# Thirteen edge tiles for four runs of nodes, an earlier last product and a shorter finish in a two-layer graph kernel

## The chip, the cores and the metric

The kernel runs on one core of a Trainium2 chip. A core has five engines with queues of their own: TensorE (PE in the profile, its weight loads PEld), VectorE (DVE), ScalarE (ACT), GpSimd (POOL) and SyncE (SP). They work side by side and wait for each other through semaphores. The metric is device microseconds of one execution. Before the change the median of seven runs is 2106.64 us, the lowest 2105.11 and the highest 2107.53.

## The reference, cut to what matters

Two graph layers run over 6250 nodes of 512 numbers in fp32. There are 106,250 edges: 50,000 random pairs in both directions, and one loop per node. The edges come sorted by dst.

```python
edge_index = stack([src, dst])
# layer one
agg = segment_sum((x @ W_l.T + b_l)[src], dst)
x = layernorm(x + agg / max(deg, 1) + x @ W_r.T)
# layer two, sums by src, gathers by dst
neigh = segment_sum(h[dst] @ W_neigh.T + b_neigh, src) / max(deg, 1)
z = h + relu(h @ W_self.T + b_self + neigh)
x = layernorm(h + layernorm(z) * gamma + beta)
```

The products are linear, so the kernel sums the rows of neighbours first and multiplies the mean by the weight matrix once per node.

## The kernel before, in words

Each layer works on a list of edges sorted by the node that receives. The list is cut into tiles of 128 edges: 831 in layer one, 782 in layer two (whose one loop per node is left out of the list and added from the node's own row). A *window* is a run of at most 32 nodes. The class `Sorter` cuts the windows so that a pair of them owns a fixed number of edge tiles, `PAIR = 7` in layer one and `PAIR_L = 6` in layer two: 238 and 261 windows. `place` (L470) reads each window's first node from the sorted list with selector matmuls, writes it to `lo`, checks that no window is too wide, and writes `rel`: for every edge of each tile that a window visits, the node's place in the window.

A *group* is four windows, one from each quarter of the list (`C = 4`), with 32 of the 128 partitions each; `Q` is the number of groups, 60 in layer one and 66 in layer two. A tile that two windows share is gathered once and visited by both. `gathered` (L602) issues one indirect DMA on POOL's queue per tile, 128 rows of 2 KB each, into one of ten chunks of four tiles.

`grouped` (L616) is a software pipeline over the groups, in an order written out by hand. The iteration for group g puts the gathers of group g + 1 on POOL's queue (`fetch`) and builds that group's 0/1 matrix `hot` on DVE (`match`). PE then does the first two visits of group g, the transposes of the mean of group g - 1, the product of that group's own rows (`dense` "own", into the PSUM tile `po`), visit three, the mean's product into the same `po`, the transposes of group g's own rows, the rest of the visits and the degree. DVE and ACT make the mean (`average`). `close` runs the first half of the finish of group g - 1, and `store`, in the next iteration, the second half and the store. A visit (`visits`, L721) is a matmul of a tile's `hot` columns with the gathered rows; the four windows write four different quarters of the PSUM tile `agg`, and each fp32 matmul shows as two instructions. Own rows come by SP's queue (`begin`, L709) and results leave by it (L781), but for three groups near a layer's end, whose stores are indirect DMAs on POOL's queue (L774).

`po` has one buffer in layer one and two in layer two (`bufs=1 + layer`). The finish of layer one is `finish0` (L547), that of layer two `finish1` (L559). `both` (L178 is its line) is a DVE instruction over two tensors; `spread` gives the mean and the deviation, the latter on ACT, and `normalize` applies them. Layer two's list is sorted on DVE, ACT and PE during layer one, a few steps per group (`more`).

Of the kernel before, what the change touches and what calls it, by code (L numbers as in the profile page):

```python
# [18 lines left out]
P = 128  # L19
C = 4  # L20
H = P // C
PAIR = 7
PAIR_L = 6
CHUNKS = 10
# [74 lines left out]
def kernel(  # L99
# [53 lines left out]
    last, middle = [const.tile([P, P], F32, name=n) for n in ("last", "middle")]  # L153
    for t, row in ((last, P - 1), (middle, P // 2 - 1)):
        nc.vector.tensor_scalar(t, ones, pidx, None, op0=ALU.mult)
        nc.vector.tensor_scalar(t, t, float(row), None, op0=ALU.is_equal)

# [56 lines left out]
    class Sorter:  # L214


        def __init__(self, key, val, layer, pool, ps, loops, given=None):
# [6 lines left out]
            pair = self.pair = PAIR_L if loops else PAIR  # L224
            self.half = (pair + 1) // 2
            self.vis = self.half + 1
            self.NW = (2 * self.M + pair - 1) // pair

            self.Q = (self.NW + 2 * C - 1) // (2 * C) * 2
            Q = self.Q  # L230
# [10 lines left out]
            if loops:  # L241

                a = (E - N - CAP - 1) // P
                self.row = pool.tile([P, M - a], F32, name="row")
                nc.gpsimd.iota(self.row, pattern=[[P, M - a]], base=a * P - (E - N) + LOOP,
                               channel_multiplier=1, allow_small_or_imprecise_dtypes=True)
                self.more = const.tile([P, 1], F32, name="more")
                self.parts = 2 + (M - a - 1) // (W // CAP // 2 * 2)

# [136 lines left out]
        def first_rows(self):  # L386

            n = 1 + self.half
            self.first = const.tile([P, C, n], I32, name="first")
            for c in range(C):  # L390
                a = c * (self.Q // 2 * self.pair) - 1
                k = max(0, -a)
                v = self.val[(a + k) * P:(a + n) * P]
                nc.scalar.dma_start(self.first[:, c, k:], v.rearrange("(t p) -> p t", p=P))
# [75 lines left out]
        def place(self):  # L470

            lo, pad, Q, NW = self.lo, self.padded, self.Q, self.NW
            pair, half, vis = self.pair, self.half, self.vis
            mid = middle if pair % 2 else last
# [5 lines left out]
            ne, no = (NW + 1) // 2, NW // 2  # L480

            for a, sel, off, n in ((0, last, 0, ne), (D // 2, mid, half, no),
                                   (D, last, pair - 1, ne - 1), (D + D // 2, last, half - 1, no)):
                nc.tensor.matmul(ends[:, a:a + n], sel, bass.AP(
                    tensor=pad.tensor, offset=pad.offset + off,
                    ap=[list(pad.ap[0]), [pair, n]]), start=True, stop=True)
            nc.vector.memset(lo, float(N))
            nc.vector.tensor_copy(view(lo, (0, 2, ne, 1)), ends[:, :ne].unsqueeze(2))
            nc.vector.tensor_copy(view(lo, (1, 2, no, 1)),
                                  ends[:, D // 2:D // 2 + no].unsqueeze(2))  # L490
# [7 lines left out]
            nc.vector.tensor_tensor(bad[:, NW:NW + ne - 1].unsqueeze(2),  # L498
                                    view(one, (2, 2, ne - 1, 1)),
                                    ends[:1, D:D + ne - 1].unsqueeze(2), op=ALU.is_equal)  # L500
            nc.vector.tensor_tensor(bad[:, NW + ne - 1:2 * NW - 1].unsqueeze(2),
                                    view(one, (1, 2, no, 1)),
                                    ends[:1, D + D // 2:D + D // 2 + no].unsqueeze(2),
                                    op=ALU.is_equal)
# [7 lines left out]

            for c in range(C):
                for i, off in ((0, 0), (1, half)):
                    nodes = bass.AP(tensor=pad.tensor, offset=pad.offset + pair * Q // 2 * c + off,
                                    ap=[list(pad.ap[0]), [pair, Q // 2], [1, vis]])
                    rel = self.rel.rearrange("p (q i) v c -> p q i v c", i=2)[:, :, i, self.X:, c]
                    first = view(lo, (c * Q + i, 2, Q // 2, 1))
                    nc.vector.tensor_tensor(rel, nodes, first.to_broadcast([P, Q // 2, vis]),
                                            op=ALU.subtract)  # L520
# [26 lines left out]
    def finish0(nr, po, own, some, work):  # L547
        po = po[:nr]
        nc.vector.scalar_tensor_tensor(po, biases["bl"][:nr], some[:nr], po,
                                       op0=ALU.mult, op1=ALU.add)  # L550
        v = work.tile([P, D], F32, name="v", bufs=1)
        both(v[:nr], po, own[:nr], ALU.add)
# [6 lines left out]
    def finish1(nr, po, own, some, work):  # L559
        po = po[:nr]  # L560
        if some is None:
# [8 lines left out]
        normalize(po, po, mv, root, nr)  # L570
        both(po, po, biases["ga"][:nr], ALU.mult)
        both(po, po, biases["be"][:nr], ALU.add)
        y = work.tile([P, D], F32, name="y")
        both(y[:nr], po, own[:nr], ALU.add)
# [27 lines left out]
    def gathered(s, table, t, windows, idx):  # L602

        rows = rpool.tile([P, C, D], F32, name="rows", bufs=CHUNKS)
        got = {}
        for c in windows:
            m = c * (s.Q // 2 * s.pair) + t
            if 0 <= m < s.M:
                at = idx[:, m:m + 1] if idx is s.idx else idx[:, c, t + 1:t + 2]
                nc.gpsimd.indirect_dma_start(  # L610
# [377 lines left out]
```

## Time and profile before

| what | us |
|---|---|
| median of 7 runs | 2106.64 |
| the profiled execution | 2105.06 |
| its span | 2103.3 |
| PE busy | 1939.9 |
| POOL busy | 1556.7 |
| DVE busy | 1182.9 |
| first gather of layer one starts | 5.70 |
| last gather of layer one starts | 1063.09 |
| first gather of layer two starts | 1086.51 |
| last gather of layer two starts | 2071.27 |

The profile comes from one execution. A line of a group gives the source line, engine, operation, tiles out<-in, shapes and count; then busy us and mean ns of one; then the engine's idle time just before these instructions and what ended most of it. "issue" means that the engine waited for nothing that the profile shows. A line of the timeline gives start, duration, the instruction and its count; several like it in a row are merged (x3), and the idle time before it stands in brackets with what ended it. The granted TensorE clock was 0.987 of full speed on average.

### The profile page before, as it was taken

What the parts mean: (1) busy time and instruction counts of PE and PEld (TensorE: products, weight loads), DVE (VectorE), ACT (ScalarE), POOL (GpSimd) and SP (SyncE); (2) the same over time, 40 slices, a digit from 0 to 9 for tenths busy, and PEclk for the clock granted to TensorE, in tenths of its full rate; (3) what the DMA queues carried; (4) which work ended last, traced back from release to release, by engine and by line L of the source; (5) the groups of instructions that cost most, each with busy time, mean ns of one, the idle gap of its engine ahead of it and who ended that gap; (6) DMA issues with size and microseconds to landing.
All of it is one profiled execution on the core that took longest, in us unless ns stands there. A gap on an engine that the chain in (4) does not pass through costs nothing.

```text
span 2103.3 us, 26066 instructions
## 1 busy us (share of the span) xinstructions
PE 1939.9 (92%) x7723; PEld 669.0 (32%) x7723; DVE 1182.9 (56%) x2495; ACT 315.8 (15%) x661; POOL 1556.7 (74%) x1638
## 2 busy tenths in 40 slices
PE   4899999999999999999879999999999999999996
PEld 1333333333232333333223333333333333333332
DVE  4754555545455554343424656565656565666577
ACT  0111111111111111111101111111111111111111
POOL 7777777777777777777747777777777777777773
PEclk9999999999999999999989999999999999999999
DMA  8777777887888887777757888888888888878783
GB/s 265 229 231 240 234 238 238 239 243 232 246 252 254 252 246 240 238 241 237 232 151 225 244 243 246 245 246 243 246 244 245 246 244 244 247 243 247 242 247 116
DMA packets 186885, 498.49 MB, mean 237 GB/s; under 512 B 46562, under 2 KB 49052, under 8 KB 186726
## 3 DMA queue, kind: packets, MB, share of 16 engines
q0 software_dynamic: 130128, 426.11, 67.6%
q1 hardware_dynamic: 50228, 64.61, 9.6%
q10 hardware_dynamic: 6370, 5.94, 0.9%
q8 instruction: 65, 1.06, 0.2%
q14 instruction: 94, 0.77, 0.1%
HBM read 463.90 MB, written 32.96 MB: 236 GB/s over the span
## 4 chain that ended last, share of the span: by engine, by line
DMA 30%; POOL 28%; PE 25%; issue 14%; DVE 3%; SPq 0%; ACT 0%; POOLq 0%; ACTq 0%; DVEq 0%
POOL rows L610 28%; DMA rows<-h_d,idx 17%; DMA rows<-in_x_dram,idx 12%; PE po L599 11%; PE agg L721 10%; PE tp L591 3%; DMA rows<-in_x_dram,first 0%; DVE stats L533 0%; PE turn L296 0%; DVE po L178 0%; PE deg L730 0%; DMA first<-in_src_dram 0%; DVE agg L748 0%; DMA own<-in_x_dram,slots 0%; SPq L781 0%
## 5 line engine op out<-in xcount | busy, mean ns | idle before, releaser
L721 PE MATMUL agg<-rows,hot 128*32 128x512 f32 x4220 | 897.5, 615 | 106.4 <-DMA rows<-h_d,idx 42.4
L610 POOL DMA_INDIRECT rows<-in_x_dram,idx x815 | 783.1, 961 | 248.1 <-issue 209.3
L610 POOL DMA_INDIRECT rows<-h_d,idx x785 | 745.6, 950 | 241.5 <-issue 197.4
L599 PE MATMUL po<-wa,meanT 128*128 128x512 f32 (+1 forms) x1008 | 466.0, 605 | 0.0
L599 PE MATMUL po<-wb,ownT 128*128 128x512 f32 (+1 forms) x1008 | 453.5, 593 | 0.1
L721 PEld LDWEIGHTS agg<-rows,hot 128*32 128x32 f32 x4220 | 155.4, 109 | 625.9 <-DMA rows<-in_x_dram,idx 228.2
L582 DVE TENSOR_SCALAR inv<-deg 128x1 f32<-128x1 f32 (+1 forms) x60 | 9.5, 158 | 485.9 <-PE deg L730 478.0
L599 PEld LDWEIGHTS po<-wa,meanT 128*128 128x128 f32 (+1 forms) x1008 | 180.2, 188 | 286.7 <-issue 254.8
L599 PEld LDWEIGHTS po<-wb,ownT 128*128 128x128 f32 (+1 forms) x1008 | 180.7, 189 | 181.9 <-issue 181.6
L593 ACT COPY ownT<-tp 128x512 f32<-128x512 f32 (+1 forms) x126 | 73.2, 581 | 785.9 <-PE tp L591 776.3
L739 DVE TENSOR_SCALAR loops<-deg 128x1 f32<-128x1 f32 (+1 forms) x66 | 10.4, 158 | 310.6 <-PE deg L730 301.6
L178 DVE SCALAR_TENSOR_TENSOR srt<-srt 128x448 f32<-128x448 f32 (+3 forms) x313 | 181.1, 620 | 4.0
L752 ACT ACTIVATE mean<-agg,inv 128x512 f32<-128x512 f32 (+1 forms) x126 | 86.5, 687 | 338.9 <-DVE some L585 140.7
L661 DVE TENSOR_REDUCE hotb<-hot 128x128 bf16<-128x512 f32 (+1 forms) x126 | 133.7, 1061 | 0.1
L537 ACT ACTIVATE rstd<-mv,eps 128x1 f32<-128x1 f32 (+1 forms) x192 | 56.5, 294 | 433.8 <-DVE mv L535 430.6
L593 ACT COPY meanT<-tp 128x512 f32<-128x512 f32 (+1 forms) x126 | 73.1, 580 | 190.3 <-PE tp L591 190.3
L178 DVE SCALAR_TENSOR_TENSOR hot<-rel,cols 128x640 f32<-128x640 f32 x126 | 98.1, 778 | 0.0
L591 PEld LDWEIGHTS tp<-ident,own 128*128 128x128 f32 (+1 forms) x504 | 63.0, 142 | 79.8 <-issue 76.7
L591 PEld LDWEIGHTS tp<-ident,mean 128*128 128x128 f32 (+1 forms) x504 | 52.8, 141 | 110.9 <-issue 43.5
L591 PE MATMUL tp<-ident,own 128*128 128x128 f32 (+1 forms) x504 | 76.1, 274 | 12.2 <-DMA own<-in_x_dram,slots 6.5
L591 PE MATMUL tp<-ident,mean 128*128 128x128 f32 (+1 forms) x504 | 82.5, 287 | 4.4 <-ACT mean L752 4.4
L543 DVE TENSOR_SCALAR po<-po,mv,rstd 128x512 f32<-128x512 f32 (+1 forms) x66 | 54.0, 819 | 2.4
(152 smaller groups left out, 916.9 us busy)
## 6 DMA issues: line engine op xcount, KB each, us to landing
own<-h_d SPq DMA_DIRECT2D x261, 64.0 KB
out_dram<-y SPq DMA_DIRECT2D x250, 64.0 KB
own<-in_x_dram SPq DMA_DIRECT2D x230, 64.0 KB
h_d<-y SPq DMA_DIRECT2D x227, 64.0 KB
rows<-in_x_dram,idx POOLq DMA_INDIRECT x815
rows<-h_d,idx POOLq DMA_INDIRECT x785
wa<-in_L_gnn_W_l_dram ACTq DMA_DIRECT2D x4, 256.0 KB
wb<-in_L_gnn_W_r_dram ACTq DMA_DIRECT2D x4, 256.0 KB
```

The lines of the kernel that those rows point to most:

```text
L178: nc.vector.scalar_tensor_tensor(o, a, 1.0, b, op0=ALU.mult, op1=op)
L537: nc.scalar.activation(root[:nr], mv[:nr, 1:2], AF.Sqrt, bias=eps[:nr])
L543: nc.vector.tensor_scalar(y, v, mv[:nr, 0:1], root[:nr], op0=ALU.subtract, op1=ALU.mult)
L582: nc.vector.tensor_scalar(inv[:nr], deg, 1.0, None, op0=ALU.max)
L591: nc.tensor.transpose(p[:, k, :nr], v[:nr, k * P:(k + 1) * P], ident[:nr, :nr])
L593: nc.scalar.copy(t[:, :, :nr], p[:, :, :nr])
L599: nc.tensor.matmul(po[:nr], aT[:, k, :nr], w[:, k, :], start=first and k == 0, stop=end and k == NK - 1)
L610: nc.gpsimd.indirect_dma_start(out=rows[:, c, :], out_offset=None, in_=table, in_offset=bass.IndirectOffsetOnAxis(ap=at, axis=0))
L661: nc.vector.tensor_reduce(hb[:, 0, :], hots[g][:, s.X * C:n * C].rearrange("p (v c) h -> p (c h) v", c=C), axis=mybir.AxisListType.X, op=A ...
L721: nc.tensor.matmul(agg[H * c:H * (c + 1), :], hot[:, C * (s.X + v) + c, :], chunks[t][c], start=t == ts[0], stop=t == ts[-1])
L739: nc.vector.tensor_scalar(st["loops"][:nr], deg[:nr, 1:2], 1.0, None, op0=ALU.add)
L752: nc.scalar.mul(st["mean"][:nr], st["agg"][:nr], st["inv"][:nr])
```

## The change

In layer two four windows own 13 tiles, so that there are 241 windows in 61 groups. Layer one keeps two windows to 7 tiles and its 60 groups. In layer two the windows of a cycle begin at rows 127, 31, 63 and 95 of a tile; the first of the four visits five tiles and the others four, and since 61 is one more than a multiple of four, the four windows of a group stand at four different places of the cycle. The selector tiles become four, the copies and checks of `place` run over the places of the cycle, and `rel` has five visits per window, filled with -1 where there is none.

Gathered rows are kept in 40 tiles of their own rather than ten chunks of four. The last group of each layer issues its own rows' product at the end of its own iteration, behind its sums and after `close` of the group before, rather than in the extra iteration behind the transposes of its mean. `finish0` adds the scaled bias to the own rows in a tile `v` and then the product to it. `finish1` makes `add`, own rows plus `be`, ahead of the rest, and its affine part and the last sum are two instructions in place of four.

```diff
-PAIR = 7
-PAIR_L = 6
-CHUNKS = 10
+CYCLE = 2, 7
+CYCLE_L = 4, 13
+ROWS = 40
...
-    last, middle = [const.tile([P, P], F32, name=n) for n in ("last", "middle")]
-    for t, row in ((last, P - 1), (middle, P // 2 - 1)):
+    row_of = {}
+    for row in range(P // 4 - 1, P, P // 4):
+        t = row_of[row] = const.tile([P, P], F32, name=f"row{row}")
         nc.vector.tensor_scalar(t, ones, pidx, None, op0=ALU.mult)
         nc.vector.tensor_scalar(t, t, float(row), None, op0=ALU.is_equal)
+    last = row_of[P - 1]
...
-            self.NW = (2 * self.M + pair - 1) // pair
-
-            self.Q = (self.NW + 2 * C - 1) // (2 * C) * 2
-            Q = self.Q
+            n, T = self.cycle = CYCLE_L if loops else CYCLE
+            self.NW = (n * self.M + T - 1) // T
+
+            Q = self.Q = (self.NW + C - 1) // C
+
+
+            starts = [i * T * P // n - 1 for i in range(n + 1)]
+            self.at = [v // P for v in starts[:n]]
+            self.row_at = [v % P for v in starts[:n]]
+            self.num = [b // P - a // P + 1 for a, b in zip(starts, starts[1:])]
+            self.vis = max(self.num)
...
+        def tiles(self, w):
+
+            k, i = divmod(w, self.cycle[0])
+            a = k * self.cycle[1] + self.at[i]
+            return range(a, a + self.num[i])
...
+            if Q % n:
+                nc.vector.memset(self.rel, -1.0)
             for c in range(C):
-                for i, off in ((0, 0), (1, half)):
...
+                for i in range(n):
+                    g = (i - c * Q) % n
+                    k = (Q - g + n - 1) // n
+                    w = c * Q + g
...
+                    rel = self.rel[:, g::n, self.X:self.X + self.num[i], c]
...
     def finish0(nr, po, own, some, work):
-        po = po[:nr]
-        nc.vector.scalar_tensor_tensor(po, biases["bl"][:nr], some[:nr], po,
+        v = work.tile([P, D], F32, name="v", bufs=1)
+        nc.vector.scalar_tensor_tensor(v[:nr], biases["bl"][:nr], some[:nr], own[:nr],
                                        op0=ALU.mult, op1=ALU.add)
-        v = work.tile([P, D], F32, name="v", bufs=1)
-        both(v[:nr], po, own[:nr], ALU.add)
+        both(v[:nr], po[:nr], v[:nr], ALU.add)
...
     def finish1(nr, po, own, some, work):
         po = po[:nr]
+        add = work.tile([P, D], F32, name="add", bufs=1)
+        both(add[:nr], own[:nr], biases["be"][:nr], ALU.add)
...
         yield
-        normalize(po, po, mv, root, nr)
-        both(po, po, biases["ga"][:nr], ALU.mult)
-        both(po, po, biases["be"][:nr], ALU.add)
+        nc.vector.reciprocal(root[:nr], root[:nr])
+        nc.vector.scalar_tensor_tensor(po, po, mv[:nr, 0:1], biases["ga"][:nr],
+                                       op0=ALU.subtract, op1=ALU.mult)
         y = work.tile([P, D], F32, name="y")
-        both(y[:nr], po, own[:nr], ALU.add)
+        nc.vector.scalar_tensor_tensor(y[:nr], po, root[:nr], add[:nr],
+                                       op0=ALU.mult, op1=ALU.add)
...
-    def gathered(s, table, t, windows, idx):
-
-        rows = rpool.tile([P, C, D], F32, name="rows", bufs=CHUNKS)
...
+    def fetched(s, table, g, chunks, idx):
+
+
+        for v in range(0 if g == 0 else 1, s.vis):
+            for c in range(C):
+                w = c * s.Q + g
+                m = s.tiles(w)[v:v + 1]
+                if w < s.NW and m and 0 <= m[0] < s.M:
+                    rows = chunks[w, v] = rpool.tile([P, D], F32, name="rows", bufs=ROWS)
+                    at = idx[:, m[0]:m[0] + 1] if idx is s.idx else idx[:, c, v:v + 1]
+                    nc.gpsimd.indirect_dma_start(
+                        out=rows, out_offset=None, in_=table,
+                        in_offset=bass.IndirectOffsetOnAxis(ap=at, axis=0))
+                if w < s.NW and v == 1 and g:
+                    t = s.tiles(w - 1)
+                    chunks[w, 0] = chunks[w - 1, len(t) - 1]
...
             def match(g):
                 hot = work.tile([P, (s.X + s.vis) * C, H], F32, name="hot")
-                n = (s.X + len(visit_tiles(g))) * C
+                n = (s.X + most(g)) * C
...
-                for v, t in list(enumerate(visit_tiles(g)))[some]:
+                for v in range(s.vis)[some]:
                     for c in windows(g):
-                        ts = [u for u in visit_tiles(g) if c in chunks[u]]
-                        if t in ts:
+                        w = c * Q + g
+                        have = [u for u in range(s.vis) if (w, u) in chunks]
+                        if v in have:
                             nc.tensor.matmul(agg[H * c:H * (c + 1), :],
                                              hot[:, C * (s.X + v) + c, :],
-                                             chunks[t][c], start=t == ts[0], stop=t == ts[-1])
+                                             chunks[w, v], start=v == have[0], stop=v == have[-1])
...
                 if g:
                     turn(g - 1, "mean")
-                    dense(g - 1, "own")
+                    if g < Q:
+                        dense(g - 1, "own")
...
                 if g:
                     close(g - 1)
+                if g == Q - 1:
+                    dense(g, "own")
```

## Prediction

> **What bounds the kernel now.** I read the page's engine line first, then the groups of instructions, the waits, and last the timelines of POOL and DVE side by side.
>
> ```profile
> PE 1939.9 (92%) x7723; PEld 669.0 (32%) x7723; DVE 1182.9 (56%) x2495; ACT 315.8 (15%) x661; POOL 1556.7 (74%) x1638
> ...
> L610 POOL DMA_INDIRECT rows<-in_x_dram,idx x815 | 783.1, 961 | 248.1 <-issue 209.3
> L610 POOL DMA_INDIRECT rows<-h_d,idx x785 | 745.6, 950 | 241.5 <-issue 197.4
> ```
>
> PE at 92% looks like the bound, but its matmuls stretch while they wait for rows. POOL shows only 74%, yet its gathers (0.96 and 0.95 us) and the idle time just before them (0.30 us each) add up to 783.1 + 248.1 + 745.6 + 241.5 = 2018 of 2103 us. The waits say what that idle time is:
>
> ```profile
> POOL rows L610 <- issue: 412.2, 1354, 0.3
> PEld agg L721 <- DMA rows<-in_x_dram,idx: 228.2, 272, 2.2
> PEld agg L721 <- DMA rows<-h_d,idx: 180.9, 176, 2.2
> POOL rows L610 <- DMA rows<-in_x_dram,idx: 25.6, 84, 0.3
> ```
>
> The columns are total us, times, longest. No gather ever waited over 0.3 us: POOL issues one gather per 1.25 us without a pause, and PE waits for rows. In the second layer the first gather starts at 1086.51 and the last at 2071.27: 984.76 us less one store of 1.33 is 983.43 for 784 steps, 1.254 each. So the time is a POOL chain of 834 + 785 gathers, plus what lies outside it: the end of layer one (last gather 1063.09 to 1086.51) and the end of the kernel (2071.27 to 2103.3).
>
> What lengthens one gather is seen where POOL and DVE run together. First two DVE operations with both inputs in SBUF, then one with an input in PSUM:
>
> ```profile
> 430.10 1.81 DVE L178 SCALAR_TENSOR_TENSOR srt<-srt 128x448 f32<-128x448 f32 x3
> 430.80 1.27 POOL L610 DMA_INDIRECT rows<-in_x_dram,idx  x1 [0.30 <-DMA rows<-in_x_dram,idx]
> ...
> 1087.52 0.68 DVE L178 SCALAR_TENSOR_TENSOR bs_t<-bs_t,bn_t 128x512 f32<-128x512 f32 x1
> 1087.82 1.22 POOL L610 DMA_INDIRECT rows<-h_d,idx  x1 [0.30 <-issue]
> ...
> 2044.60 0.69 DVE L178 SCALAR_TENSOR_TENSOR po<-po,bs_t 128x512 f32<-128x512 f32 x1
> 2044.86 0.95 POOL L610 DMA_INDIRECT rows<-h_d,idx  x1 [0.30 <-issue]
> ```
>
> The gather at 1087.82 started 0.30 us into bs_t<-bs_t,bn_t, which ended at 1088.20, and took 1.22 instead of 0.945. The one at 2044.86 started inside po<-po,bs_t (po is PSUM) and took 0.95. I counted all gathers that start at least 0.06 us after a DVE operation began and 0.15 before its end: under srt<-srt 33 of 33 are long, 7.35 us together; under operations with one PSUM input 1 of 227. The excess is, nearly exactly, the operation's end minus the gather's start minus 0.125 us (this gives 7.39 for the 33). Nothing absorbs it: it shifts every later gather.
>
> **The change, part by part.** It is summed against the profiled execution, 2105.06 us (span 2103.3 and 1.8 around it); that is 1.58 under the median 2106.64, and differences carry over.
>
> *61 groups for 66.* The gathers stay 782 + 3 = 785, so at 1.254 us the POOL chain of layer two keeps its 984 us. A group now has 13 gathers (16.3 us) for 12 (15.0). PE saves five groups' products and transposes, and 20 own loads and 20 stores go from SP's queue: cost nothing and gain nothing, since PE already waits. In each group one window has a fifth visit, alone in its round. The trace has no such lone matmul pair at full pace; between nothing (if other strips hide it) and 1.04 us (the last pair at 2001.90) I take 0.87, two passes at the 0.43 spacing of the po weight loads. PE's group from 1506.20 to 1521.41 has 5.0 us for visits that take 1.92 when rows are there, so it needs 12.1, and 13.0 after, against 16.3. The cover is 3.3 us. hot grows from 20 to 24 columns and hotb by a quarter (0.16 + 0.25 us of DVE); DVE has about 11 us of work per group and loses a 0.7 us operation in the finish.
>
> *Rows in 40 tiles for 10 chunks of four.* Same bytes; a gather's buffer is 40 gathers old either way, whose group PE finished some 27 us before. More gathers carry a wait of their own: those named after a DMA or PE above kept the same 0.30 us gap, so nothing; the rival below prices it.
>
> *Selector tiles and placing.* Four more DVE operations of 0.29 and 0.23 us ahead of the first fills: 1.0 us on the path to idx, which is ready at 27.07, while POOL wants it at 30.16. Place for layer two runs at 905 to 912 us, long before its use; its extra copies and smaller subtracts cost at most one lengthened gather, 0.4 us, taken as 0.
>
> *Last group's own product earlier.* It moves eight PE instructions and no DMA, past PE's transpose of the mean only. Layer one has one po buffer: the product still waits for v of the group before (1071.9), and now the transpose of the mean, its ACT copy and the load, which hid behind it, come after: 0.55 + 0.1 + 0.48 = 1.1 us later. Finish0 no longer adds the bias to po after the last product, 0.78 less. Sum +0.36. Layer two has two po buffers: the product starts at 2080.3 instead of 2082.81. But the mean's copy on ACT is queued behind rstd of the group before, itself 0.73 later for the new add on DVE: copy done 2085.4, mean product done 2089.1; DVE is free of the former group's finish and of the last group's own add at 2089.28, where it started at 2089.88: -0.60.
>
> *Finish of the last group.* One scale (0.85 with its gap) and three steps of 0.73 become two steps of 0.73: 3.04 - 1.46 = -1.58.
>
> *Backlog at the end of layer two.* Before, PE's last sums end 8.8 us after the last gather's start (2080.06 less 2071.27); groups 63 to 65 take PE 12.37, 12.19 and 12.38 against nine gathers (11.3 us, once 12.6 with a store). At group 62, of 11 gathers, it was 7.07. Group 57 has 11 too; then three groups of ten gathers (12.54) and PE 0.87 longer: 7.07 + 0.70 + 0.52 - 0.81 (the store) = 7.48: -1.31. With the lone visit hidden it would be -3.9; at 1.04 us, -0.8.
>
> *Operations with two SBUF inputs.* This is what decides. Finish0's bias step reads bl_t and po today; it will read bl_t and own, both SBUF: 60 times. Finish1 gets add<-own,be_t, both SBUF: 61 times. The steps that go (the scale, ga, be, own) all read po in PSUM and held no gather. An operation of 0.69 us holds a gather that starts 0.06 to 0.56 us into it, for 0.50 down to 0: 0.125 us² over a pitch of 1.25, 0.10 us each at random phase. For layer one the phase is known, since the step keeps its place behind inv and some: laid over the gathers of the trace, 30 of the 60 would be held, 6.2 us. Sliding it by up to 0.75 us gives 3.7 to 9.8. In layer two add takes the place of po<-po,bs_t, but the lone visit moves the phase: over a whole pitch I get 1.3 to 9.8, mean 6.0. I take +6.2 and +6.0, the ends for the range. In the other direction, five y steps fewer (3.2 us of holding over 66) give -0.25.
>
> Sum: +0.36 - 0.60 - 1.58 - 1.31 - 0.25 + 12.2 = +8.8: 2113.9 for a profiled run, 2115.4 for the median.
>
> [...]
>
> **Rivals.** Under 0.2% (4.2 us) no change can be told.
> - *The new steps hold no gather.* No row has two SBUF inputs and a scalar read from a tile, as finish0's step does. Then only -3.4 is left: 2103.2. The bs_t row, of the same form as add, speaks against it. This is the case that is not slower; it decides when the 119 steps that meet gathers cost under 0.06 us each (7.2 us, which leaves less than 4.2).
> - *Five groups fewer shorten the layer.* Five times 15.0 us: 2031. It needs PE as the bound; the 0.3 us waits exclude it nearly.
> - *Each gather pays for its own wait.* If a wait showed as 0.05 us on some 1,200 more gathers, +60: 2175. Equal gaps speak against it.
> - *The lone visit makes PE the bound* if it costs over 3.3 us. At 4.3 it would be +61: 2176; no matmul row is near that.
>
> **How the numbers follow.** The forecast's case has 0.86, of which 0.06 falls within 0.2% (both layers at the low ends: 5.0 of holding); steps that hold nothing 0.07 (0.05 same, 0.02 faster with the larger backlog gain); fewer groups 0.02, faster; own waits 0.03 and lone visit 0.02, slower. So slower 0.85, same 0.11, faster 0.04. Range: 5.0 - 3.4 is +1.6, 2108; 19.6 - 3.4 is +16.2, 2123.
>
> **What would show it.** Mean gather about 969 ns in layer one (961 before) and 958 in layer two (950), with long gathers under v<-bl_t,some,own and add<-own,be_t; gather count 785; pitch, not group count, setting layer two's length. Last gather of layer one to first of layer two about 23.8 us (23.4 before); last gather to the last store's start 23.3 (26.84). Wrong if gathers under the new steps stay at 0.945, or POOL shows waits over 0.3.

## The result, and the profile after

The changed kernel takes 2112.44 us (median of 15 runs, 2106.37 to 2116.28) against 2106.64 for the kernel before (36 runs, 2103.80 to 2109.95): a ratio of 1.0027, interval 1.0021 to 1.0034. It is 5.8 us slower. The profiled execution took 2110.17 us, its span is 2108.4; against the 2103.3 of before that is +5.1, and this is the difference taken apart below.

First the page of the changed kernel, its engine line and the two groups of gathers (busy us, mean ns, idle just before):

```profile
PE 1960.0 (93%) x7561; PEld 662.7 (31%) x7561; DVE 1106.0 (52%) x2356; ACT 302.1 (14%) x631; POOL 1562.7 (74%) x1638
...
L635 POOL DMA_INDIRECT rows<-in_x_dram,idx x815 | 787.6, 966 | 248.0 <-issue 114.7
L635 POOL DMA_INDIRECT rows<-h_d,idx x785 | 747.3, 952 | 241.6 <-issue 118.2
```

Work has become less (162 fewer PE instructions, 77 us less DVE), and the time has grown. The number of gathers is the same and the idle time before them too; what grew is the gather itself, by 5 ns in layer one and 2 ns in layer two. Its waits, in us in total, times and longest:

```profile
POOL rows L635 <- issue: 238.4, 783, 0.3
PEld agg L742 <- DMA rows<-in_x_dram,idx: 232.5, 285, 2.3
PEld agg L742 <- DMA rows<-h_d,idx: 232.1, 292, 2.6
...
POOL rows L635 <- PE agg L742: 79.5, 261, 0.3
POOL rows L635 <- DMA rows<-in_x_dram,idx: 70.1, 230, 0.3
POOL rows L635 <- DMA rows<-h_d,idx: 67.6, 222, 0.3
```

Of all 1619 gathers (the 19 of layer one's start included) 836 now have something other than issue named as their releaser, 265 before. Each of these rows still gives 0.304 to 0.305 us per gather, and but for the first gather of each layer none waited over 0.32: a wait that is already met adds nothing to the 0.30. PE still waits for rows, and POOL never rests.

The span cut at the first and last gather of each layer (from the timeline of POOL, in us):

| stretch | before | after | difference | forecast |
|---|---|---|---|---|
| start to first gather | 5.70 | 5.65 | -0.05 | 0 |
| gathers of layer one | 1057.39 | 1061.62 | +4.23 | +6.2 |
| last gather of layer one to first of layer two | 23.42 | 26.83 | +3.41 | +0.36 |
| gathers of layer two | 984.76 | 986.56 | +1.80 | +5.75 |
| last gather to the end | 32.02 | 27.74 | -4.29 | -3.49 |
| sum | 2103.30 | 2108.40 | +5.1 | +8.8 |

The two gather stretches can be checked in another way: sum what each gather takes above 0.945 us. In layer one that is 13.61 us before and 17.86 after (+4.25), in layer two 3.74 and 5.52 (+1.78). The stretches grew by what the gathers grew, and by nothing else.

**A gather held in layer one.** From the timeline (start, duration, engine, line, operation); v<-bl_t,some,own is finish0's new first step, both tensors in SBUF:

```profile
1061.62 0.74 DVE L570 SCALAR_TENSOR_TENSOR v<-bl_t,some,own 128x512 f32<-128x512 f32 x1
...
1062.09 1.09 POOL L635 DMA_INDIRECT rows<-in_x_dram,idx  x1 [0.30 <-DMA rows<-in_x_dram,idx]
...
1063.48 0.95 POOL L635 DMA_INDIRECT rows<-in_x_dram,idx  x1 [0.30 <-issue]
```

The step ends at 1062.36, 0.27 us after the gather began; 0.27 less 0.125 is 0.145, and the gather took 1.09 instead of 0.945. Of 33 gathers that meet this step (here and below: that start at least 0.06 us into a step and 0.125 before its end) 29 are long, 8.21 us together. Each of the 29 follows the rule to 0.01 us. Three of the other four began 0.06 to 0.09 us into the step and took 0.94 to 0.95; the earliest of the long ones began 0.18 us into it. (The fourth is held by only 0.01.)

**A gather missed in layer two**, under the new step add<-own,be_t, from the same view:

```profile
1511.40 0.95 POOL L635 DMA_INDIRECT rows<-h_d,idx  x1 [0.30 <-issue]
1511.77 0.69 DVE L180 SCALAR_TENSOR_TENSOR add<-own,be_t 128x512 f32<-128x512 f32 x1
...
1512.37 0.69 DVE L180 SCALAR_TENSOR_TENSOR po<-po,bs_t 128x512 f32<-128x512 f32 x1
1512.66 0.95 POOL L635 DMA_INDIRECT rows<-h_d,idx  x1 [0.30 <-PE agg L742]
```

The add begins 0.37 us after one gather did and is over, at 1512.46, 0.20 us before the next. Nothing is held. 46 of the 61 adds begin 0.1 to 0.6 us after a gather did and miss the next one, and none of those 46 gathers took over 0.95 us. Only 7 gathers meet an add, 6 of them long, 1.87 us in all.

**The end of layer one.** The timeline's lines of PE before the change, from the transposes of the last group's mean on:

```profile
1071.31 0.55 PE L591 MATMUL tp<-ident,mean 96*128 96x96 f32 x4 [1.24 <-ACT mean L752]
...
1071.95 3.67 PE L599 MATMUL po<-wb,ownT 128*96 128x512 f32 x8
```

And in the changed kernel, from the last group's own product on:

```profile
1077.36 5.34 PE L622 MATMUL po<-wb,ownT 128*96 128x512 f32 x8 [1.97 <-DVE v L180]
...
1082.54 0.50 PE L614 MATMUL tp<-ident,mean 96*128 96x96 f32 x4
...
1083.66 3.67 PE L622 MATMUL po<-wa,meanT 128*96 128x512 f32 x8 [0.62 <-ACT meanT L616]
```

This stretch of the changed kernel in windows: length, busy us and count of PE, PEld, DVE, ACT and POOL, then granted clock, DMA share and GB/s:

```profile
1075.00:1077.30 2.30, 0.39 (x4) 0.12 (x1) 1.77 (x6) 0.68 (x1) 0.00 (x0) 1.00 0.00 0
1077.30:1079.30 2.00, 1.94 (x3) 0.81 (x4) 1.53 (x5) 0.29 (x1) 0.00 (x0) 0.59 0.00 0
1079.30:1082.50 3.20, 3.20 (x6) 1.04 (x5) 0.73 (x1) 0.00 (x0) 0.00 (x0) 0.72 0.27 64
```

The product of the kernel before, in one window of its own trace:

```profile
1071.90:1075.70 3.80, 3.75 (x9) 1.55 (x10) 1.57 (x4) 0.66 (x2) 0.00 (x0) 1.00 0.10 25
```

Same eight matmuls, 5.34 us for the first product and 3.67 for the second: the granted clock in the two windows of the first is 0.59 and 0.72. They come after PE stood idle for 1.97 us, waiting for v of the group before. In the kernel before the transposes of the mean stood between, PE's pause was 1.24 us, and the product ran at full clock.

The clock records of the traces say when it was halved. In this trace the granted clock changes 15 times and in that of the kernel before 13 times, in each at moments that lie a whole number of 3.41 us apart (here 1077.66, 1081.08, 1091.32 and 1101.56 us, and 1074.25 by counting back). Between 1074.25 and 1077.66, where the whole pause lies, PE was busy for 1.44 us; over the next 3.41 us the clock was one half:

```profile
1074.25:1077.66 3.41, 1.44 (x9) 0.46 (x9) 2.13 (x6) 1.16 (x2) 0.00 (x0) 1.00 0.06 23
1077.66:1081.07 3.41, 3.41 (x5) 1.14 (x4) 1.90 (x5) 0.29 (x1) 0.00 (x0) 0.50 0.11 28
```

**The end of the kernel.** Timeline, last gather to last store:

```profile
2080.66 0.95 POOL L635 DMA_INDIRECT rows<-h_d,idx  x1 [0.31 <-issue]
...
2087.68 0.25 PE L751 MATMUL deg<-ones_b,hotb 128*96 128x1 bf16 x2
...
2087.79 3.65 PE L622 MATMUL po<-wb,ownT 128*96 128x512 f32 x8
...
2092.82 3.67 PE L622 MATMUL po<-wa,meanT 128*96 128x512 f32 x8 [1.04 <-ACT meanT L616]
...
2103.24 0.94 POOL L795 DMA_INDIRECT out_dram<-y,slots  x1 [20.30 <-DVE y L564]
```

The last sums (deg follows them) are done 7.02 us after the last gather began, 8.79 before (deg at 2080.06, last gather at 2071.27). The own product starts at once behind them. The finish, from its last bias step at 2096.59 to the store, is 6.65 us long, 8.23 before.

### The profile page after: what moved, and what is told of

Read it like the earlier page. It is cut to its first block, busy times and chain, and to the rows that moved or that the text cites. A ratio compares the mean times of both kernels' runs of the same rounds, so it can differ in the third digit from the quotient of the medians.

```text
span 2108.4 us, 26520 instructions
## 1 busy us (share of the span) xinstructions
PE 1960.0 (93%) x7561; PEld 662.7 (31%) x7561; DVE 1106.0 (52%) x2356; ACT 302.1 (14%) x631; POOL 1562.7 (74%) x1638
## 4 chain that ended last, share of the span: by engine, by line
PE 47%; DMA 35%; issue 8%; POOL 7%; DVE 2%; ACT 0%; POOLq 0%; SPq 0%; ACTq 0%; DVEq 0%
PE po L622 24%; PE agg L742 19%; DMA rows<-h_d,idx 17%; DMA rows<-in_x_dram,idx 17%; POOL rows L635 7%; PE tp L614 4%; DMA rows<-in_x_dram,first 0%; PE deg L751 0%; PE turn L469 0%; PE turn L308 0%; DMA first<-in_src_dram 0%; DMA own<-in_x_dram,slots 0%; PE turn L498 0%; DVE stats L554 0%; DVE v L180 0%
## 5 line engine op out<-in xcount | busy, mean ns | idle before, releaser
L742 PE MATMUL agg<-rows,hot 128*32 128x512 f32 x4180 | 953.7, 615 | 94.4 <-DMA rows<-in_x_dram,idx 38.6
L622 PE MATMUL po<-wa,meanT 128*128 128x512 f32 (+1 forms) x968 | 447.6, 605 | 1.7 <-ACT meanT L616 1.7
L622 PE MATMUL po<-wb,ownT 128*128 128x512 f32 (+1 forms) x968 | 437.8, 595 | 2.0 <-DVE v L180 2.0
L742 PEld LDWEIGHTS agg<-rows,hot 128*32 128x32 f32 x4180 | 165.9, 109 | 667.8 <-DMA rows<-in_x_dram,idx 232.5
L622 PEld LDWEIGHTS po<-wa,meanT 128*128 128x128 f32 (+1 forms) x968 | 172.8, 188 | 276.3 <-issue 239.9
L622 PEld LDWEIGHTS po<-wb,ownT 128*128 128x128 f32 (+1 forms) x968 | 174.2, 190 | 177.9 <-issue 175.9
L681 DVE TENSOR_REDUCE hotb<-hot 128x128 bf16<-128x640 f32 x121 | 142.7, 1179 | 0.1
L180 DVE SCALAR_TENSOR_TENSOR hot<-rel,cols 128x768 f32<-128x768 f32 (+1 forms) x121 | 102.3, 845 | 0.0
L614 PE MATMUL tp<-ident,own 128*128 128x128 f32 (+1 forms) x484 | 73.1, 274 | 10.7 <-DMA own<-in_x_dram,slots 6.4
L596 DVE SCALAR_TENSOR_TENSOR y<-po,rstd,add 128x512 f32<-128x512 f32 (+1 forms) x61 | 45.8, 751 | 2.1
```

What stands on the lines that cost most here:

```text
L180: nc.vector.scalar_tensor_tensor(o, a, 1.0, b, op0=ALU.mult, op1=op)
L596: nc.vector.scalar_tensor_tensor(y[:nr], po, root[:nr], add[:nr], op0=ALU.mult, op1=ALU.add)
L614: nc.tensor.transpose(p[:, k, :nr], v[:nr, k * P:(k + 1) * P], ident[:nr, :nr])
L622: nc.tensor.matmul(po[:nr], aT[:, k, :nr], w[:, k, :], start=first and k == 0, stop=end and k == NK - 1)
L681: nc.vector.tensor_reduce(hb[:, 0, :], hots[g][:, s.X * C:n * C].rearrange("p (v c) h -> p (c h) v", c=C), axis=mybir.AxisListType.X, op=A ...
L742: nc.tensor.matmul(agg[H * c:H * (c + 1), :], hot[:, C * (s.X + v) + c, :], chunks[w, v], start=v == have[0], stop=v == have[-1])
```

## The experiments

Theory: the slowdown is gathers held by the two new steps whose inputs are both in SBUF; how much each layer pays is a matter of phase. Rivals: the new steps cost nothing, and the loss is what the earlier own product does at the end of layer one; or the new windows cost. Four kernels ran together, beside a kernel before of 2104.58 us (21 runs).

**No two-SBUF step in the finishes.** In the changed kernel finish0 gets its old first two steps back, and finish1 reads be from a copy in PSUM.

```diff
 def finish0(nr, po, own, some, work):
-    v = work.tile([P, D], F32, name="v", bufs=1)
-    nc.vector.scalar_tensor_tensor(v[:nr], biases["bl"][:nr], some[:nr], own[:nr],
+    po = po[:nr]
+    nc.vector.scalar_tensor_tensor(po, biases["bl"][:nr], some[:nr], po,
                                    op0=ALU.mult, op1=ALU.add)
-    both(v[:nr], po[:nr], v[:nr], ALU.add)
+    v = work.tile([P, D], F32, name="v", bufs=1)
+    both(v[:nr], po, own[:nr], ALU.add)
...
+    be_sbuf = biases["be"]
+    biases["be"] = ps.tile([P, D], F32, name="be_p")
+    nc.vector.tensor_copy(biases["be"], be_sbuf)
...
```

> The changed kernel, but no DVE step that meets gathers has both inputs in SBUF: finish0 is the one of before, and finish1's add reads be from a copy in PSUM. Theory (two SBUF inputs hold gathers): the 8.2 us under v<-bl_t,some,own and the 1.9 us under add<-own,be_t go, the bias step of layer one comes back behind the last product (+0.8): 2112.4 - 10.1 + 0.8 = 2103.1, give or take 2.5 us for other holds that change phase; no gather long under add. Rival (the new buffers, waits and groups cost the time, or the order at the end of layer one does): the finish is off the path, so 2112 to 2113.

Measured: 2105.99 us (11 runs), ratio 0.9999, interval 0.9990 to 1.0008 (the two medians alone give 1.0007). The slowdown is gone; the rest of the change taken together (windows, earlier own product, shorter finish1) makes no difference that can be told. Its parts cancel: the end of layer one is 26.31 us here for 23.42 before, the end of the kernel 28.83 for 32.02. From this kernel's page:

```profile
L636 POOL DMA_INDIRECT rows<-in_x_dram,idx x815 | 785.7, 964 | 248.0 <-issue 120.8
L636 POOL DMA_INDIRECT rows<-h_d,idx x785 | 745.4, 950 | 241.5 <-issue 133.8
```

And from its timeline, the own product at the end of layer one:

```profile
1076.01 3.65 PE L623 MATMUL po<-wb,ownT 128*96 128x512 f32 x8 [1.97 <-DVE v L180]
```

A gather that starts inside the add, which now reads be from PSUM:

```profile
1509.05 0.68 DVE L180 SCALAR_TENSOR_TENSOR add<-own,be_p 128x512 f32<-128x512 f32 x1
1509.26 0.95 POOL L636 DMA_INDIRECT rows<-h_d,idx  x1 [0.30 <-DMA rows<-h_d,idx]
```

No gather is long under add or under finish0's bias step. Yet layer one's gathers are only 1.9 us shorter than in the changed kernel, where v alone held 8.2: all gathers that start under srt<-srt are held for 10.7 us here and 6.6 there. With layer two's the gathers are 3.9 us shorter and the profiled span 3.3, less than the 0.28% (5.9 us) between the two ratios; these profiles are one execution each.

The own product, after the same pause of 1.97 us, runs at full pace. Counted back from this trace's change of clock at 1088.72, one of the moments 3.41 us apart falls inside the pause, at 1075.07, and PE is busy for 2.39 and 2.47 us on its two sides:

```profile
1071.65:1075.07 3.42, 2.39 (x14) 0.80 (x12) 0.96 (x4) 1.00 (x2) 0.00 (x0) 1.00 0.13 51
1075.07:1078.48 3.41, 2.47 (x6) 1.06 (x7) 2.33 (x6) 0.45 (x2) 0.00 (x0) 1.00 0.00 0
```

The rival that the steps hold nothing falls; the forecast for this kernel, 2103.1, was 2.9 too low.

**The add one step later.** In the changed kernel the add moves behind the bias step, 0.7 us later; the work is the same.

```diff
-        both(add[:nr], own[:nr], biases["be"][:nr], ALU.add)
         if some is None:
...
             both(po, po, biases["bs"][:nr], ALU.add)
+        both(add[:nr], own[:nr], biases["be"][:nr], ALU.add)
```

> The changed kernel with add<-own,be_t one DVE step (0.73 us) later, behind the bias step; same instructions. Theory: in the changed kernel's trace add starts mostly 0.13 to 0.6 us after a gather does, so that only 7 of 61 hold the next; slid by 0.75 us over the same gathers, 37 would hold one, 12.0 us for 1.9. So +10: 2122.5, and layer two's mean gather goes from 952 to about 965 ns. Rival (the hold has no part in it, DVE is off the path): 2112.4, mean gather 952.

Measured: 2119.74 us (5 runs), ratio 1.0069, interval 1.0055 to 1.0083, which is 0.42% above the changed kernel's ratio. A line pair of its timeline:

```profile
1530.73 0.68 DVE L180 SCALAR_TENSOR_TENSOR add<-own,be_t 128x512 f32<-128x512 f32 x1
1530.81 1.43 POOL L635 DMA_INDIRECT rows<-h_d,idx  x1 [0.30 <-PE agg L742]
```

From its page, the second layer's gathers:

```profile
L635 POOL DMA_INDIRECT rows<-h_d,idx x785 | 756.6, 964 | 241.6 <-issue 113.9
```

All 34 gathers that meet the add are long, 11.01 us (the rule gives 11.05; one more, 0.04 us into the step, was held for 0.5), and layer two's gathers take 995.81 us for 986.56, +9.25. Nothing but the moment of one 0.68 us step was changed. This settles why layer two paid little in the changed kernel: phase.

**Both new finishes alone**, in the kernel before: 66 groups, old windows, old order.

```diff
 def finish0(nr, po, own, some, work):
...
+    nc.vector.scalar_tensor_tensor(v[:nr], biases["bl"][:nr], some[:nr], own[:nr],
+                                   op0=ALU.mult, op1=ALU.add)
+    both(v[:nr], po[:nr], v[:nr], ALU.add)
...
 def finish1(nr, po, own, some, work):
     po = po[:nr]
+    add = work.tile([P, D], F32, name="add", bufs=1)
+    both(add[:nr], own[:nr], biases["be"][:nr], ALU.add)
...
```

> The kernel before with the two new finishes alone. Theory: layer one's hold comes whole, 6.2 (laid over the trace of before) to 8.2 us (measured in the changed kernel); in layer two add stands where po<-po,bs_t stood in groups of 12, where laid over the trace it would hold 36 gathers for 8.5 us; the ends are shorter by 0.8 and 1.6. So +12 to +14: 2119 to 2121. Rival (finishes are off the path): -2.4, 2104.2.

Measured: 2114.68 us (5 runs), ratio 1.0047, interval 1.0034 to 1.0061; +10.1 where 12 to 14 were expected. The profiled execution, 2118.36, was the slowest of the five. From its page:

```profile
L612 POOL DMA_INDIRECT rows<-in_x_dram,idx x815 | 791.1, 971 | 248.1 <-issue 208.3
L612 POOL DMA_INDIRECT rows<-h_d,idx x785 | 752.0, 958 | 241.8 <-issue 203.0
```

v holds 8.84 us (28 of 31 gathers) and add 6.68 (31 of 32). The finishes alone lose more than the whole change does (10.1 us for 5.8), without a new window or a moved product.

**The earlier own product alone**, in the kernel before.

```diff
                 if g:
                     turn(g - 1, "mean")
-                    dense(g - 1, "own")
+                    if g < Q:
+                        dense(g - 1, "own")
...
+                if g == Q - 1:
+                    dense(g, "own")
```

> The kernel before with the last group's own product at the end of its iteration, alone. Theory: at the end of layer one the product still waits for po, and the transpose and copy of the mean come behind it (+1.1); PE idle for 2 us may bring the half clock on the product that the changed kernel shows (+1.7); the end of layer two gains 0.4, since DVE is busy with the former group's finish to 2089.46. So +0.7 to +2.4: 2107.3 to 2109.0. Rival (the order makes the whole of the loss): 2112. Rival (it gains at both ends): 2104.

Measured: 2106.15 us (11 runs), ratio 1.0010, interval 1.0001 to 1.0019. It costs about 2 us (0.2 to 4 by the interval), as expected in size. Its timeline at the end of layer one:

```profile
1070.38 5.34 PE L599 MATMUL po<-wb,ownT 128*96 128x512 f32 x8 [1.97 <-DVE v L178]
```

Two windows over that product, columns as before:

```profile
1070.30:1072.30 2.00, 1.92 (x3) 0.74 (x4) 1.53 (x4) 0.29 (x1) 0.00 (x0) 0.66 0.00 0
1072.30:1075.50 3.20, 3.20 (x6) 1.11 (x5) 0.00 (x0) 0.00 (x0) 0.00 (x0) 0.68 0.26 64
```

The end of layer one is 26.56 us here for 23.42, without any other part of the change, and the half-clocked product is in it again. It was seen in three of the four kernels that take the product early at this place: the changed one, the one with the later add, and this one. In the changed one the whole pause lies between two of the moments 3.41 us apart, PE is busy for 1.44 us between them, and the clock is one half for the next 3.41 us. Here the two windows, at 0.66 and 0.68, hold 1.36 and 2.05 us of half clock if the rest is at full, together 3.41 again, from about 1070.94 on, with the whole pause in the 3.41 us before. In the one without two-SBUF steps a moment cuts the pause. No run moved the pause alone to test whether that decides. In the trace of the changed kernel, from its first clock record on, PE was busy for at most 1.49 us in the 3.41 us ahead of each of the eight halvings, and for 1.60 or more in every other such stretch at full clock. In the kernel before, six of the seven halvings follow 1.32 us or less, but one follows 2.04 (at 906.37), and PE was busy for 1.53 us between two such moments (2080.55 to 2083.96), with a pause in it, where the clock stayed at 1.00.

What every gather takes above 0.945 us, summed by layer, over the six kernels (us; one profiled execution each):

| kernel | layer one | of it under v | layer two | of it under add |
|---|---|---|---|---|
| before | 13.61 | - | 3.74 | - |
| own product early, alone | 11.62 | - | 2.58 | - |
| no two-SBUF step | 15.97 | - | 3.55 | - |
| changed | 17.86 | 8.21 | 5.52 | 1.87 |
| add later | 16.90 | 6.17 | 14.75 | 11.01 |
| finishes alone | 21.61 | 8.84 | 10.17 | 6.68 |

The three with the new finish0 average 18.8 us in layer one, the three without 13.7: v is worth about 5, less than the 6 to 9 under it, and what v does not hold scatters by 4 us from kernel to kernel, for the sorting steps' phase moves too.

**Other chips.** The remaining kernels ran on two other chips, where the kernel before itself took 2488.73 us (25 runs) and 2510.01 (17 runs). Four ran on the first of them. One is the changed kernel with the finishes and the order of before, to see the windows alone (and the rows in 40 tiles).

```diff
 def finish0(nr, po, own, some, work):
-    v = work.tile([P, D], F32, name="v", bufs=1)
...
 def finish1(nr, po, own, some, work):
     po = po[:nr]
-    add = work.tile([P, D], F32, name="add", bufs=1)
-    both(add[:nr], own[:nr], biases["be"][:nr], ALU.add)
...
-                    if g < Q:
-                        dense(g - 1, "own")
+                    dense(g - 1, "own")
...
-                if g == Q - 1:
-                    dense(g, "own")
```

> The changed kernel with both finishes and the order of before: only 13 tiles for four windows, 61 groups and the rows in 40 tiles. Theory (POOL's pitch bounds both layers, the hold comes from the finishes): layer two's chain stays at 984 us, the backlog at its end falls by about 1.3 to 1.8 us, so -1 to -2 against the kernel before; ratio 0.999 to 1.000, mean gathers about 961 and 950 ns. Rival (five groups fewer shorten the layer): up to -75. Rival (a wait for each gather): +60 or more, and gaps over 0.30 us.

Measured: 2502.13 us, ratio 1.0053, interval 1.0034 to 1.0073.

The second keeps the parts that the kernels above left as worth having: be in PSUM, the new finish0 for the last group of layer one alone, the earlier product in layer two alone.

```diff
...
-                st["finish"] = finish(st["nr"], st["po"], st["own"], st["some"], work)
+                end = g == Q - 1 and not s.loops
+                st["finish"] = (finish0_end if end else finish)(
+                    st["nr"], st["po"], st["own"], st["some"], work)
...
-                    if g < Q:
+                    if g < Q or not s.loops:
                         dense(g - 1, "own")
...
-                if g == Q - 1:
+                if g == Q - 1 and s.loops:
                     dense(g, "own")
```

> The changed kernel with what costs taken out: be read from PSUM, finish0 of before in all groups but the last, which meets no gather, and the last group's own product early in layer two alone. Theory: chains as before; the end of layer one 0.8 shorter; the end of the kernel 3.2 to 4.3 shorter. So -4 to -5 against the kernel before, ratio 0.9976 to 0.9981. Rival (the windows have a cost of their own at the end of layer one, where three kernels with the new buffers took 0.4 to 1.7 us longer from the last gather to the degree): -2.5 to -4, 0.9981 to 0.9988.

Measured: 2500.88 us, ratio 1.0048, interval 1.0032 to 1.0064.

The last two put dead work into the finishes of before: two steps each that nobody reads, with both inputs in SBUF, or, in the twin, with one in PSUM.

```diff
 def finish0(nr, po, own, some, work):
+    for _ in range(2):
+        both(work.tile([P, D], F32, name="dead", bufs=1)[:nr], biases["bl"][:nr], own[:nr], ALU.add)
...
 def finish1(nr, po, own, some, work):
     po = po[:nr]
+    for _ in range(2):
+        both(work.tile([P, D], F32, name="dead", bufs=1)[:nr], biases["be"][:nr], own[:nr], ALU.add)
```

The twin reads `po` in place of `biases["bl"]` and `biases["be"]`.

> The kernel before with two dead DVE steps at the start of each finish, own plus bl_t or be_t into a tile that nobody reads: both inputs in SBUF. Theory: laid over the gathers of the trace of before, the first steps hold 6.2 us in layer one and 8.5 in layer two, the second, 0.75 us later, 4.8 and 2.2: +22 (15 to 25), ratio 1.007 to 1.012, most of it in longer gathers. Rival (DVE time is what costs): the same as with the twin whose first input is in PSUM.

> The twin: the same two dead steps with po, in PSUM, in place of bl_t or be_t. Theory: no gather is held; each layer's end is longer by two steps of 0.73 us, which now wait for the last product: +2.9, ratio 1.0014, mean gathers 961 and 950 ns. Rival (DVE time is what costs): the same as with both inputs in SBUF.

Measured: 2500.00 us, 1.0043 (1.0027 to 1.0058), and 2497.63, 1.0031 (1.0018 to 1.0043). The pair of lines that tells most is one where both kernels happen to have the same phase, a gather 0.34 us into the first dead step. Timeline of the kernel with SBUF steps:

```profile
1516.29 1.41 DVE L178 SCALAR_TENSOR_TENSOR dead<-be_t,own 128x512 f32<-128x512 f32 x2
1516.63 1.16 POOL L614 DMA_INDIRECT rows<-h_d,idx  x1 [0.30 <-issue]
```

Timeline of its twin:

```profile
1509.25 1.41 DVE L178 SCALAR_TENSOR_TENSOR dead<-po,own 128x512 f32<-128x512 f32 x2
1509.59 0.95 POOL L614 DMA_INDIRECT rows<-h_d,idx  x1 [0.30 <-issue]
```

1.16 against 0.95, the same operation with one input elsewhere. One such step alone takes 0.69, so the first of the two ends 0.35 us after the gather's start, and 0.35 less 0.125 is the 0.22 that it took longer; the second step, which starts later, adds nothing. In all, 105 of the 107 gathers that meet a dead SBUF step are long, 24.4 us; under the PSUM steps none is by more than 0.03. But the time hardly shows it: the two intervals overlap. The waits of the kernel with SBUF steps say why:

```profile
POOL rows L614 <- issue: 435.0, 1415, 4.1
...
POOL rows L614 <- remote: 172.4, 67, 6.2
...
POOL rows L614 <- PE agg L725: 167.7, 66, 11.2
```

And one line of the waits of the kernel with the windows alone:

```profile
POOL rows L633 <- PE agg L740: 196.2, 125, 11.1
```

POOL waits for PE to give buffers back, up to 11 us, and about as long in all for a releaser that the trace calls remote and does not name further; where the kernel before takes 2105 us no gather inside a layer waited over 0.32. A held gather then seems to be taken from POOL's idle time. The hold showed as time only where POOL never rests.

The same four kernels once more, on the second of the two chips:

> The same kernel as chosen_parts, whose chip took 2488.7 us for the kernel before, with PE idle for reasons that the trace does not name and POOL waiting up to 11 us. Theory: where the kernel before takes about 2105 us, POOL's pitch bounds the layers, and -4 to -5 remains to be seen: ratio 0.9976 to 0.9981. Rival (the windows cost 0.4 to 1.7 us at the end of layer one): 0.9981 to 0.9988. Where it takes about 2490 again: 1.003 to 1.006, as seen.

> The same kernel as windows_only. Theory, on a chip where the kernel before takes about 2105 us: ratio 0.999 to 1.000, layer two's chain 984 us with 61 groups, as with 66. Rival (fewer groups shorten it): below 0.99. Rival (each gather pays a wait): above 1.02. On a chip of 2490 us: 1.003 to 1.007, as seen.

> The same kernel as two_sbuf_steps. There the dead steps held 105 gathers for 24.4 us, and yet the time was only 0.12% over the twin's, where POOL was not the bound. Theory, on a chip of 2105 us: held gathers add up, +15 to +25 us, ratio 1.007 to 1.012, and the twin stays at 1.001 to 1.002. Rival (the hold never adds up whole): within 0.2% of the twin.

> The twin again. Theory, on a chip of 2105 us: +2.9 us at the two ends, ratio 1.0014, mean gathers 961 and 950 ns. Rival (DVE time is what costs): as two_sbuf_again.

Measured against 2510.01 us: 2533.12 (1.0080, 1.0059 to 1.0100) for the chosen parts, 2534.58 (1.0097, 1.0078 to 1.0115) for the windows alone, 2517.62 (1.0027, 1.0017 to 1.0038) with SBUF steps, 2523.27 (1.0051, 1.0033 to 1.0070) with PSUM steps. There 105 of 108 gathers are long under the SBUF steps, 25.8 us, and that kernel is the faster of the two.

So what these eight runs expected for a chip where POOL never rests was not tested. Two of them also said what a slow chip would show, 1.003 to 1.006 for the chosen parts and 1.003 to 1.007 for the windows alone; the measured 1.0080 and 1.0097 lie above both. What stays open: what the windows alone cost or bring on such a chip; whether the chosen parts beat the kernel before there, for no run shows it (on the other two chips they are 0.5% and 0.8% slower); why the windows cost 0.5 to 1% on the other chips; and why those chips take 18 to 19% more.

## Why the prediction was right, and where it was not

The forecast was 2115.4 (2108 to 2123) and slower; measured are 2112.44 and slower. The mechanism was the one named, and the kernel without it is back at the time of before. By the steps:

- *POOL bounds, PE does not; 61 groups for 66 gain nothing.* Right. Layer two's gathers take 986.56 us for 984.76, and the difference is all in the length of the gathers.
- *Rows in 40 tiles: own waits cost nothing.* Right: 0.304 to 0.305 us per gather whoever releases it. The rival at 2175 fell with that.
- *Lone visit on PE, cover 3.3 us.* Right that it is covered: no gather waits over 0.3 us. The rival at 2176 fell.
- *Operations with two SBUF inputs, layer one: +6.2, ends 3.7 and 9.8.* Right in kind. Under v itself 8.2 us were held, near the upper end, while what gathers lost under srt<-srt went from 8.8 us to 6.6 and under y from 1.44 to 0.32: +4.23 in all. The prediction took what other steps hold as fixed, and it moves with the phase.
- *The same, layer two: +6.0, ends 1.3 and 9.8.* The term that was mis-sized most: 1.87. A mean over a whole pitch was taken for a step whose phase is not spread evenly: 46 of 61 adds fall into the 0.5 us where they meet no gather. One step later it was 11.0, with the old windows 6.7. The three values span the range that was given, and the last goes past its upper end; which one would come depends on a phase that the trace of before does not have.
- *Five y steps fewer: -0.25.* Failed: y<-y,mv,rstd held 2.15 us before (not 3.2, which is what the rule gives for the 19 gathers that meet it: 3 of them were not held) and 3.27 after, +1.12, by phase again.
- *Last group's own product earlier, layer one: +0.36.* Failed: the end of layer one grew by 3.41. The two parts that it named are there: transposes and copy behind the product 1.12 (1.1 forecast), the shorter finish -0.79 (-0.78). It left out that PE, without the transposes in front, pauses 1.97 us and that the product then ran at 0.59 to 0.72 of the clock: its eight matmuls' starts span 4.75 us for 3.08, +1.67. Another 1.14 us is between the last gather and the last sums' end (7.91 for 6.77), and three short waits give the remaining 0.27. The kernels with the new windows and row tiles have 7.91, 8.45 and 7.16 from gather to sums, those with the old ones 6.77, 6.94 and 6.97, so it goes with one of these; which and how was not shown, and layer one's own windows are the same in all six.
- *Layer two: -0.60.* -0.91 from the sums' end to the last bias step.
- *Finish of the last group: -1.58.* 8.23 to 6.65 us, -1.58.
- *Backlog: -1.31.* -1.77. The forecast holds a slip: by its own rows the last of the three groups gives 12.38 + 0.87 - 13.87 = -0.62, not -0.81, so the sum is -1.12. Other kernels with the same windows have 7.60 and 8.10 us in place of 7.02, and the finishes alone, with the old windows, 7.68, so how much of the gain the windows give is not shown.
- *The new steps hold no gather (0.07, 2103.2).* Fell by the 29 of 33 and 34 of 34 long gathers, and by 1.0027 (from 1.0021) against 0.9999 (to 1.0008).

The misses partly cancelled: layer two's gathers grew 4 us less and layer one's 2 us less than forecast, layer one's end 3 us more. That the total came within 4 us is in part luck.

## What to carry to other kernels

Where one engine issues without a pause, count what every other engine's step does to that issue before counting work saved: here a step of 0.68 us, off the path in all groups but a layer's last, held gathers for up to 11 us because both of its inputs were in SBUF. Keep one input in PSUM (under the twin's dead steps no gather was longer by more than 0.03 us), or put the step right behind a gather's start (46 of 61 adds stood there by chance and held nothing; it was not tried on purpose), and expect such a cost to come and go with phase, so that any edit which shifts the timing can turn it up or down by several us. When work is moved, look at what filled the engine's pauses before, and at the granted clock behind the pause that opens (0.59 and 0.72 here, behind 1.97 us).

## What the runs showed that I had not expected

- The hold is exact: each long gather under v follows the rule (step's end, less the gather's start, less 0.125 us) to 0.01 us. How far into the step a gather must begin differs: under v the latest that was not held began at 0.09 us and the earliest held at 0.18, under the y steps of the two kernels 0.14 and 0.16, under srt<-srt 0.03 and 0.03.
- Two SBUF tensors are not the only form that holds. The y steps (TENSOR_SCALAR, one SBUF tensor and two columns of scalars) held gathers too, 1.44 us in layer one and 2.15 in layer two of the kernel before, while hotb<-hot (TENSOR_REDUCE, one SBUF tensor) lengthened 1 of the 49 gathers that met it in layer one of the changed kernel.
- Eight matmuls took 5.34 us where 3.65 is usual, after a pause of PE of 1.97 us, in three kernels of four that had this pause.
- The same program took 2105 us on one chip and 2489 and 2510 on two others. There the granted clock averaged 0.87 to 0.89 instead of 0.99, POOL waited for buffers, and ACT began its copy of a transposed tile of own rows 3.4 to 4.7 us after PE had ended the transposes (the medians of the eight kernels), 0.04 on the first chip. On those chips some 25 us of lengthened gathers did not make a kernel slower than its twin beyond the noise.
